# Spreading the output units of a graph-attention kernel over more of its edge steps, and a drain on GpSimd

## The chip, the cores and the metric

The kernel runs on one core of one Trainium2 chip. The core's engines are TensorE (PE, with its weight loads shown as PEld), VectorE (DVE), ScalarE (ACT), GpSimd (POOL) and SyncE (SP, which here only issues DMAs); each works through its own queue in order, and the queues meet through semaphores. The metric is the device time of one execution in microseconds (us), given as the median of several runs.

## The reference

One layer of graph attention over 12,500 nodes and 400,000 edges, with the edges sorted by their target node. The targets are dense at low node numbers: node index grows as the square of the place in the edge list, so half of the edges go to the first quarter of the nodes.

```python
h   = relu(layernorm(x))
msg = (h @ w_src + b_src)[src] + (h @ w_dst)[dst]            # E x 128
rad = mlp3(edge_attr_32)                                     # 32 -> 64 -> 64 -> 128, silu
msg = (msg * edge_weight * rad) @ w_sep + b_sep              # 8 heads x (16 alpha + 16 value)
score = einsum(smooth_leaky_relu(alpha), alpha_dot)          # E x 8
att   = segment_softmax(score, dst)
agg   = segment_sum(value * att, dst)                        # 12500 x 128
out   = x + agg @ w_proj + b_proj
```

## The kernel before, in words

**Setup.** `x` is normalised and multiplied by the two node matrices, and the tables `t_src` and `t_dst` are stored to DRAM (line L335). Meanwhile SP loads weights and a few single words of `dst`: `load_limits` (L243 to L251) fetches, among others, one word per output unit. From these the kernel finds out whether every node of a unit is complete when the unit is begun; if not, it takes a slow path that sorts the edges.

**Edge steps.** The edges are cut into 782 sections of 512, and two sections make a step `k`; there are 391 of them (`NP`), followed by 12 steps that only empty the pipeline. The function `step(k)` issues, in an order written out by hand, pieces of many pipeline stages: the loads of edge weights, targets and target rows some steps ahead; the gathers of step `k+2` on GpSimd (`gather`, L1013: eight indirect DMAs, each with the `t_src` rows of 128 edges); the MLP of steps `k+1` and `k+2`; in step `k` TensorE's transposes of the gathered rows (`sources`, L1073), the multiplication by the radial weights (`radial`, L1062, once in each step, and `message`, L1090); the scores of step `k-1`; the softmax of groups of eight steps (at `k % 8` of 2 and 3); and for step `c = k-12` (`LAG`) the weighted values (L1228), their sums by node (`sums`, L1241 and L1245) and SP's stores of the sums to DRAM (`store`, L1253, into `agg`; `store_win`, L1249). Every 32 steps a "block" repairs nodes that are split between sections (lines L1361 to L1436). The gathers have five buffers for each section of a step (`GSB`), so GpSimd can be three steps ahead of TensorE before it has to wait for a buffer.

**Output units.** The final stage (quotient, projection, residual) is cut into 23 units of 512 nodes (`UNITS`, `UNIT`). Unit `u` begins at step `306 + 4u` (`U0`), the last at step 394, and is spread over three steps: at `q = 0` SP loads its rows of `agg` and of `x` (`load_unit`, L1298; `load_x`, L1303); at `q = 1` VectorE adds the bias and forms the quotients (`unit_bias`, `unit_quotients`, L1307 to L1315); at `q = 2` TensorE transposes (`unit_turn`, L1321, with ScalarE's copy L1323), multiplies by `w_proj` (`unit_product`, L1329), VectorE adds `x` (`unit_out`, L1335) and SP stores the rows of `out` (L1336). The transposes and the product use the PSUM bank `m1`, which the MLP, the scores and the softmax of the same step also use. The buffers of a unit (`gu`, `xs`, `qT`, `ru`) are single.

**The end.** Behind the last gathers of `t_src`, GpSimd gathers rows of `x` for the last 13 steps (`rows_dx`, L1455), loads the block results (L1636, L1638), adds the bias (L1642) and gathers further rows of `x` (`rows_x`, L1449). Its next work is the scatter of finished rows to `out` (`direct_scatter`, L1282; `scatter`, L1440). The first of these scatters is issued only behind the store of the last unit, in step 396 (`late_out`), since it overwrites rows that the units have written.

Of the kernel before, what the change touches and what calls it, by code (L numbers as in the profile page):

```python
# [21 lines left out]
P = 128  # L22
# [16 lines left out]
SEC = T * TS  # L39
# [6 lines left out]
AHEAD = 13  # L46
UNIT = 512
UNITS = 23
U0 = 306
DIRECT = 13  # L50
GSB = 5

# [2 lines left out]
def gnn_kernel(ctx: ExitStack, tc: tile.TileContext, a: dict, out: bass.AP):  # L55
    nc = tc.nc
    x, src, dst = a["x"], a["src"], a["dst"]
    ea, ew = a["edge_attr_32"], a["edge_weight1"]
    N, E = x.shape[0], src.shape[0]
# [3 lines left out]
    NS = -(-E // SEC)  # L63
# [25 lines left out]
    def done(k):  # L89

        return 2 * (k - LAG - 2) + 2

    D = NP - DIRECT
    IN_AGG = done(U0 + 4 * (UNITS - 1)) // 2
    assert D < IN_AGG and done(U0 + 4 * (UNITS - 1)) < NS and UNITS * UNIT + P * 4 >= N - UNIT
    NF = N // P
    tail = N - NF * P
    assert NB == NF + 1
# [80 lines left out]
    with tc.tile_pool(name="node", bufs=2) as np_, tc.tile_pool(name="node1", bufs=1) as n1, \  # L179
# [57 lines left out]
        lim = n1.tile([1, UNITS + 3], I32, name="lim")  # L237
# [5 lines left out]
        def load_limits():  # L243

            with nc.allow_non_contiguous_dma(reason="single targets"):
                at = dst[done(U0) * SEC:done(U0) * SEC + 1]
                nc.sync.dma_start(out=lim[:, 0:UNITS], in_=bass.AP(at.tensor, at.offset, [[1, 1], [8 * SEC, UNITS]]))
                nc.sync.dma_start(out=lim[:, UNITS:UNITS + 1], in_=dst[EARLY * SEC:EARLY * SEC + 1].unsqueeze(0))
                nc.sync.dma_start(out=lim[:, UNITS + 1:UNITS + 2],
                                  in_=dst[(NS - 1) * SEC:(NS - 1) * SEC + 1].unsqueeze(0))  # L250
                nc.sync.dma_start(out=lim[:, UNITS + 2:UNITS + 3], in_=dst[2 * D * SEC:2 * D * SEC + 1].unsqueeze(0))  # L251
# [297 lines left out]
        for i in range(Q):  # L549
# [12 lines left out]
            if i == 1:  # L562
                load_targets()
                load_limits()
# [20 lines left out]
        for i in range(Q - 10, Q):  # L585
            q = i - (Q - 10)
# [321 lines left out]
    def windows():  # L908
# [7 lines left out]
        with tc.tile_pool(name="ps", bufs=1, space=PSUM) as pp, \  # L916
# [33 lines left out]
            def prep_make(u):  # L950
                ri, rb = made[u]
                rows = lp.tile([P, P], F32, name="rows", bufs=1)
                rf = lp.tile([P, 1], F32, name="rf", bufs=1)
                nc.vector.tensor_copy(rf, rb)
                nc.vector.tensor_copy(rows[:T, :], ri[:T, 0, :])
                rel[u] = sp.tile([P, T], F32, name="rel")
                nc.vector.tensor_scalar(rel[u], ri[:, 1, 0:T], rf, None, op0=ALU.subtract)
                made[u] = rows
# [179 lines left out]
            def load_sm(m):  # L1138
                sms[m] = sp.tile([MQ, SEC + 1], BF16, name="sm")
                at = same[0:1, m * MQ * SEC:m * MQ * SEC + 1]  # L1140
                nc.sync.dma_start(out=sms[m], in_=bass.AP(at.tensor, at.offset, [[SEC, MQ], [1, SEC + 1]]))
# [106 lines left out]
            def store_win(c):  # L1248
                nc.sync.dma_start(out=win[c * P:(c + 1) * P, :], in_=accs[c])  # L1249

            def store(c, f):
                at = nc.sync.value_load(base[0:1, f, c:c + 1])
                nc.sync.dma_start(out=agg[ds(at, W - 1), :], in_=accs[c][f * W:(f + 1) * W - 1, :])  # L1253
# [90 lines left out]
            def width(g):  # L1344
                return min(P, NE - g * P)
# [101 lines left out]
            def rows_x(g):  # L1447
                w = width(g)
                nc.gpsimd.indirect_dma_start(  # L1449
                    out=xe_at(g)[:w, :], out_offset=None, in_=x[:, :],  # L1450
                    in_offset=bass.IndirectOffsetOnAxis(ap=ids[:w, g:g + 1], axis=0),
                    bounds_check=N - 1, oob_is_err=False)
# [12 lines left out]
            def xe_at(g):  # L1465
                return big["xe", g // TS][:, g % TS, :]
# [9 lines left out]
            def has(k):  # L1476
                return 0 <= k < NP
# [7 lines left out]
            def step(k):  # L1485
                c = k - LAG
                if has(c - 2) and k <= NP:
                    store_win(c - 2)
                    if c - 2 < IN_AGG:
                        store(c - 2, 0)  # L1490
# [11 lines left out]
                if has(k) and k % MP == 4:  # L1502
                    load_sm(k // MP)
                if has(c - 2) and k <= NP and c - 2 < IN_AGG:
                    store(c - 2, 1)
# [3 lines left out]
                    prep_make(0)  # L1509
                if k % 16 == 7 and has(k + 9):  # L1510
                    prep_make((k + 9) // 16)
                u, q = divmod(k - U0, 4)
                unit = 0 <= u < UNITS
                if unit and q == 0:
                    load_unit(u, sp)
                    load_x(u, sp)
# [40 lines left out]
                if has(c - 1):  # L1557
                    sums(c - 1)
                    if k >= NP:
                        if k == NP + LAG:  # L1560
                            last_rows_2()
                        else:
                            store_win(c - 1)
                        if c - 1 < IN_AGG:
                            store(c - 1, 0)
# [52 lines left out]
            for k in range(-5, NP):  # L1618
                step(k)
                if k == NP - 4:  # L1620
                    block_load(last - 1)
                if k == NP - 2:
                    block_maxima(last - 1)
                    block_nodes(last)
                if k == NP - 1:
                    block_factors(last - 1)
# [6 lines left out]
            for c in range(D, NP):  # L1633
# [3 lines left out]
                                in_=obs_d[0:g0 * P, :].rearrange("(g p) c -> p g c", p=P))  # L1637
            nc.gpsimd.dma_start(out=big["ye", 1][:, 0:(last - 1 - g0) * C].rearrange("p (g c) -> p g c", c=C),  # L1638
                                in_=obs_d[g0 * P:(last - 1) * P, :].rearrange("(g p) c -> p g c", p=P))
            for i in range(-(-DIRECT // TS)):  # L1640
                n = min(TS, DIRECT - i * TS)
                nc.gpsimd.tensor_tensor(big["xw", i][:, 0:n, :], big["xw", i][:, 0:n, :],  # L1642
                                        b_out.unsqueeze(1).to_broadcast([P, n, C]), op=ALU.add)
            for g in range(NC):
                rows_x(g)

            def sum_rows():
                for g in range(0, last - 1, TS):
                    n = min(TS, last - 1 - g)
                    v = big["ye", g // 8][:, g % 8 * C:(g % 8 + n) * C].rearrange("p (g c) -> p g c", c=C)  # L1650
                    nc.gpsimd.tensor_tensor(v, v, big["xe", g // TS][:, 0:n, :], op=ALU.add)
# [31 lines left out]
            for k in range(NP, NP + LAG + 1):  # L1683
                step(k)
                if k - NP in jobs:
                    jobs[k - NP]()
# [83 lines left out]
    with tc.If(unfit == 0) as fit:  # L1770
        windows()
# [70 lines left out]
```

## Time and profile before

| | us |
|---|---|
| median of 3 runs | 4093.39 |
| lowest, highest run | 4090.29, 4094.85 |
| the profiled execution | 4088.26 |
| its span, first to last instruction | 4086.4 |
| PE busy | 3863.1 (95%) |
| DVE busy | 3100.8 (76%) |
| POOL busy | 3061.4 (75%) |
| ACT busy | 1864.5 (46%) |

The profiled execution is 5.1 us below the median and has 1.9 us around its span. In the profile each group of instructions has a line of the kernel, an engine, the tile written and the tiles read, a count, the busy time and the mean time of one, and then the idle time of the engine in front of it with what ended that idle time. "issue" is time in which the engine waited for nothing that the profile shows. The timeline gives start and duration of single instructions in us from the span's start. The line "L1013 ... x3021" counts the gathers into the tiles `gs`; 72 further gathers of the first steps go into other buffers.

### The profile page before, as it was taken

What the parts mean: (1) busy time and instruction counts of PE and PEld (TensorE: products, weight loads), DVE (VectorE), ACT (ScalarE), POOL (GpSimd) and SP (SyncE); (2) the same over time, 40 slices, a digit from 0 to 9 for tenths busy, and PEclk for the clock granted to TensorE, in tenths of its full rate; (3) what the DMA queues carried; (4) which work ended last, traced back from release to release, by engine and by line L of the source; (5) the groups of instructions that cost most, each with busy time, mean ns of one, the idle gap of its engine ahead of it and who ended that gap; (6) DMA issues with size and microseconds to landing.
All of it is one profiled execution on the core that took longest, in us unless ns stands there. A gap on an engine that the chain in (4) does not pass through costs nothing.

```text
span 4086.4 us, 84243 instructions
## 1 busy us (share of the span) xinstructions
PE 3863.1 (95%) x27811; PEld 2347.4 (57%) x27811; DVE 3100.8 (76%) x5557; ACT 1864.5 (46%) x3782; POOL 3061.4 (75%) x3244
## 2 busy tenths in 40 slices
PE   7899999999999999999999999999999999999996
PEld 6356555655555555555555555555555565555555
DVE  7677777777777777777777777777777788777876
ACT  5454444444454444444444444444444444444441
POOL 6777777777777777777777777777777777777775
PEclk9999999999999999999999999999999999999998
DMA  7777777777677776776767676777767777777761
GB/s 248 209 189 195 178 199 189 182 189 185 183 177 190 186 185 169 193 191 173 184 184 189 172 187 186 189 177 186 183 180 191 200 202 200 200 205 202 197 183 53
DMA packets 536556, 762.20 MB, mean 187 GB/s; under 512 B 126721, under 2 KB 339747, under 8 KB 535984
## 3 DMA queue, kind: packets, MB, share of 16 engines
q1 hardware_dynamic: 378120, 498.27, 41.9%
q0 software_dynamic: 101872, 207.34, 24.0%
q10 hardware_dynamic: 56120, 51.10, 4.4%
q8 instruction: 226, 3.70, 0.4%
q14 instruction: 218, 1.79, 0.2%
HBM read 632.27 MB, written 125.70 MB: 185 GB/s over the span
## 4 chain that ended last, share of the span: by engine, by line
PE 66%; DMA 11%; POOL 9%; issue 6%; DVE 5%; SPq 2%; ACT 2%; ACTq 0%; DVEq 0%; POOLq 0%
PE V L1228 14%; PE pa L1096 13%; PE misc L1241 8%; DMA gs<-t_src,idx 8%; POOL gs L1013 7%; PE p L1057 6%; PE pm L1073 6%; PE m L1029 5%; PE pm L1085 4%; PE p L1042 4%; PE m L1113 3%; POOL mT L1013 2%; DMA agg<-ob 1%; DVE mT L1090 1%; DMA win<-ob 1%
## 5 line engine op out<-in xcount | busy, mean ns | idle before, releaser
L1013 POOL DMA_INDIRECT gs<-t_src,idx x3021 | 2871.6, 951 | 922.2 <-issue 774.0
L1098 ACT ACTIVATE sl<-pa,c_b_a 128x512 f32<-128x512 f32 x782 | 537.5, 687 | 1085.1 <-PE pa L1096 1083.3
L1103 DVE SCALAR_TENSOR_TENSOR al<-pa,sl 128x512 f32<-128x512 f32 x782 | 536.8, 686 | 524.0 <-ACT sl L1098 512.3
L1228 PEld LDWEIGHTS V<-c_w_v,mT 128*128 128x128 f32 x6154 | 755.4, 193 | 300.8 <-DVE ob L1245 124.1
L1228 PE MATMUL V<-c_w_v,mT 128*128 128x128 f32 x6154 | 888.0, 288 | 0.0
L1096 PE MATMUL pa<-mT,c_w_a 128*128 128x512 f32 x1564 | 835.1, 616 | 20.9 <-DVE mT L1090 18.6
L1230 DVE TENSOR_TENSOR pvx<-V,Pem 128x512 f32<-128x512 f32 x770 | 528.4, 686 | 222.3 <-PE V L1228 206.6
L1073 PEld LDWEIGHTS pm<-ident,gs 128*128 128x128 f32 x3021 | 373.6, 141 | 495.5 <-issue 470.1
L1044 ACT ACTIVATE h<-p,b 128x512 f32<-128x512 f32 x391 | 469.2, 1200 | 399.5 <-PE p L1042 332.9
L1062 DVE SCALAR_TENSOR_TENSOR rad<-p,c_fc_b,w_b 128x1024 f32<-128x1024 f32 x391 | 500.8, 1281 | 122.2 <-PE p L1057 105.0
L1073 PE MATMUL pm<-ident,gs 128*128 128x128 f32 x3021 | 458.1, 274 | 76.9 <-DMA gs<-t_src,idx 76.4
L1241 PEld LDWEIGHTS misc<-pvx,oh 128*64 128x64 f32 x6250 | 352.4, 137 | 295.9 <-ACT h L1032 286.5
L1090 DVE SCALAR_TENSOR_TENSOR mT<-pm,c_b_src,rad 128x1024 f32<-128x1024 f32 x391 | 497.5, 1272 | 7.1 <-PE pm L1085 6.3
L1241 PE MATMUL misc<-pvx,oh 128*64 128x136 f32 x6250 | 452.2, 287 | 0.4 <-ACT h L1032 0.3
L1057 PE MATMUL p<-h,w3b 64*128 64x512 f32 x1564 | 408.6, 600 | 0.4 <-ACT h L1044 0.4
L1029 PE MATMUL m<-eT,w1b 64*128 64x256 f32 x782 | 277.3, 435 | 19.7 <-ACT qT L1323 14.2
L1085 PE MATMUL pm<-ohT,m 64*128 64x512 f32 x1564 | 287.7, 446 | 0.0
L1032 ACT ACTIVATE h<-misc,b 128x256 f32<-128x256 f32 x391 | 185.4, 474 | 214.4 <-PE misc L1029 198.5
L1029 PE MATMUL misc<-eT,w1b 64*128 64x256 f32 x782 | 277.3, 435 | 0.0
L1096 PEld LDWEIGHTS pa<-mT,c_w_a 128*128 128x128 f32 x1564 | 237.4, 192 | 68.3 <-DVE mT L1090 36.6
L1129 ACT ACTIVATE Sp<-m,b_s 128x512 f32<-128x512 f32 x192 | 131.8, 686 | 311.5 <-PE m L1113 311.5
L1042 PE MATMUL p<-h,w2b 64*64 64x256 f32 x3128 | 261.5, 405 | 0.5 <-DVE rad L1062 0.5
(216 smaller groups left out, 3542.0 us busy)
## 6 DMA issues: line engine op xcount, KB each, us to landing
w_b<-in_edge_weight SPq DMA_DIRECT2D x390, 512.0 KB
d_b<-in_dst SPq DMA_DIRECT2D x390, 256.0 KB
e_t<-in_edge_attr ACTq DMA_DIRECT2D x386, 128.0 KB
sc_d<-Sp SPq DMA_DIRECT2D x192, 256.0 KB
gs<-t_src,idx POOLq DMA_INDIRECT x3021
win<-ob SPq DMA_DIRECT2D x390, 68.0 KB
agg<-ob SPq DMA_DIRECT2D x762, 33.5 KB
md<-t_dst SPq DMA_DIRECT2D x782, 32.0 KB
```

The lines of the kernel that those rows point to most:

```text
L1013: sent = [nc.gpsimd.indirect_dma_start(out=gs[:, t, :], out_offset=None, in_=t_src[:, :], in_offset=bass.IndirectOffsetOnAxis(ap=idx[:, t0 ...
L1029: nc.tensor.matmul(p1[f], w1b[s, :], eTs[k][s, :], start=True, stop=True)
L1057: nc.tensor.matmul(p3[:, f, 0:SEC], w3b[s, :], h2s[k][s, :], start=True, stop=True)
L1062: nc.vector.scalar_tensor_tensor(rad[:, 0:n], p3.rearrange("c f e -> c (f e)")[:, 0:n], b3, w_g[k][:, 0:n], op0=ALU.add, op1=ALU.mult)
L1073: turned = [nc.tensor.matmul(pm[:, t * T:(t + 1) * T], gs[:, t, :], ident, start=(t == 0), stop=False, is_transpose=True, skip_group_check ...
L1090: nc.vector.scalar_tensor_tensor(mTs[k][:, 0:n], pms.rearrange("c f e -> c (f e)")[:, 0:n], b_n, rad[:, 0:n], op0=ALU.add, op1=ALU.mult)
L1096: nc.tensor.matmul(pa[:, 0:n], w_a, mTs[k][:, f * SEC:f * SEC + n], start=True, stop=True)
L1098: nc.scalar.activation(sl[:, 0:n], pa[:, 0:n], AF.Silu, bias=b_a, scale=1.0)
L1103: nc.vector.scalar_tensor_tensor(al, pa, 0.25, sl, op0=ALU.mult, op1=ALU.add)
L1228: nc.tensor.matmul(V[:, t, :], mTs[c][:, o:o + T], w_v, start=True, stop=True)
L1230: nc.vector.tensor_mul(pvx[c][:, f, 0:n, 0:C].rearrange("p t (h k) -> p t h k", h=H), V[:, 0:n, :].rearrange("p t (h k) -> p t h k", h=H), ...
L1241: nc.tensor.matmul(acc[f * W:(f + 1) * W, :], ohs[c][:, f * TS + t, :], pvx[c][:, f, t, :], start=(t == 0), stop=(t == n - 1), skip_group_ ...
```

## The change

The units no longer begin at every fourth step from 306 on. Four runs of steps are given instead: 96, 128, 160 and 192; then 204 to 282 by 13; then 296 to 386 by 10; then 390 and 394. The count of units, their work and the steps of the last two or three (386, 390, 394) stay as they are. `load_limits` fetches its words with four DMAs in place of one, since the steps no longer have one stride. In the end part one `drain` is issued on GpSimd between its last gathers of `x` and what follows them.

```diff
-U0 = 306
+UNIT_RUNS = ((96, 32, 4), (204, 13, 7), (296, 10, 10), (390, 4, 2))
+UNIT_STEP = [a + i * d for a, d, n in UNIT_RUNS for i in range(n)]
...
-                at = dst[done(U0) * SEC:done(U0) * SEC + 1]
-                nc.sync.dma_start(out=lim[:, 0:UNITS], in_=bass.AP(at.tensor, at.offset, [[1, 1], [8 * SEC, UNITS]]))
+                u = 0
+                for k, d, n in UNIT_RUNS:
+                    at = dst[done(k) * SEC:done(k) * SEC + 1]
+                    nc.sync.dma_start(out=lim[:, u:u + n], in_=bass.AP(at.tensor, at.offset, [[1, 1], [2 * d * SEC, n]]))
+                    u += n
...
-                u, q = divmod(k - U0, 4)
-                unit = 0 <= u < UNITS
+                unit = k >= UNIT_STEP[0]
+                u = max((i for i, a in enumerate(UNIT_STEP) if a <= k), default=0)
+                q = k - UNIT_STEP[u]
                 if unit and q == 0:
                     load_unit(u, sp)
                     load_x(u, sp)
...
             for g in range(NC):
                 rows_x(g)
+            nc.gpsimd.drain()
```

More of the change, by code (lines that the diff above doesn't have):

```diff
@@ L93, in gnn_kernel @@
     D = NP - DIRECT
-    IN_AGG = done(U0 + 4 * (UNITS - 1)) // 2
-    assert D < IN_AGG and done(U0 + 4 * (UNITS - 1)) < NS and UNITS * UNIT + P * 4 >= N - UNIT
+    IN_AGG = done(UNIT_STEP[-1]) // 2
+    assert UNITS == len(UNIT_STEP) and min(b - a for a, b in zip(UNIT_STEP, UNIT_STEP[1:])) >= 3
+    assert D < IN_AGG and done(UNIT_STEP[-1]) < NS and UNITS * UNIT + P * 4 >= N - UNIT
     NF = N // P
```

## The prediction

> **What bounds the kernel now.** The page first: what is busy, and the group that stands on top.
>
> ```profile
> PE 3863.1 (95%) x27811; PEld 2347.4 (57%) x27811; DVE 3100.8 (76%) x5557; ACT 1864.5 (46%) x3782; POOL 3061.4 (75%) x3244
> L1013 POOL DMA_INDIRECT gs<-t_src,idx x3021 | 2871.6, 951 | 922.2 <-issue 774.0
> ```
>
> PE looks like the bound. But GpSimd's 25% of idle time is nearly all "issue", some 0.3 us ahead of each gather, so its gathers may run without a real wait. So second: the gathers of L1013 in three stretches (length, busy time, count; then clock and DMA). The first lies well before the units, the second in the middle, the third holds 20 of the 23 units.
>
> ```profile
> 282.00:864.00 582.00, 440.61 (x465) 1.00 0.73 191
> 1060.00:3060.00 2000.00, 1513.72 (x1594) 0.98 0.71 184
> 3145.00:3945.00 800.00, 605.63 (x638) 1.00 0.76 201
> ```
>
> One gather starts every 2000/1594 = 1.255 us in the second stretch, every 800/638 = 1.254 us in the third: the same pace with units and without, and 10.03 us for the eight gathers of a step. Third, the pace of the steps. L1062 runs once in each step, so first and last start over the count give it, in the first stretch, in 2260 to 3060 and in the third.
>
> ```profile
> L1062 DVE SCALAR_TENSOR_TENSOR rad<-p,c_fc_b,w_b x60: 1268/1284/1285, 289.1 to 854.8; 128x1024 f32<-128x1024 f32 x60
> L1062 DVE SCALAR_TENSOR_TENSOR rad<-p,c_fc_b,w_b x80: 1266/1284/1285, 2260.8 to 3054.8; 128x1024 f32<-128x1024 f32 x80
> L1062 DVE SCALAR_TENSOR_TENSOR rad<-p,c_fc_b,w_b x79: 1264/1283/1285, 3144.8 to 3941.0; 128x1024 f32<-128x1024 f32 x79
> ```
>
> That is 565.7/59 = 9.59, 794.0/79 = 10.05 and 796.2/78 = 10.21 us a step. In the first stretch gathers made ahead are being used up, and the steps run at their own pace of 9.59. In the middle they follow GpSimd (10.03). With a unit every fourth step they follow neither: they are slower than GpSimd, and fall behind it. What PE's transposes wait for says the same; the first row is of 2260 to 3060, the second of the third stretch.
>
> ```profile
>   DMA gs<-t_src,idx: 29.8, 28
>   DMA gs<-t_src,idx: 9.1, 31
> ```
>
> How far the steps fall behind is seen from the last gather of a step and the same step's L1062. GpSimd's gathers of `t_src` end at 3973.85 with the five of step 390; counting back from there, 3957.42 is the last gather of step 388 and 2992.37 that of step 292, three 32-step block cycles before.
>
> ```profile
> 2992.37 0.94 POOL L1013 DMA_INDIRECT gs<-t_src,idx  x1 [0.30 <-issue]
> 2997.02 1.28 DVE L1062 SCALAR_TENSOR_TENSOR rad<-p,c_fc_b,w_b 128x1024 f32<-128x1024 f32 x1 [1.43 <-PE p L1057]
> 3957.42 0.94 POOL L1013 DMA_INDIRECT gs<-t_src,idx  x1 [0.30 <-issue]
> 3972.60 1.28 DVE L1062 SCALAR_TENSOR_TENSOR rad<-p,c_fc_b,w_b 128x1024 f32<-128x1024 f32 x1 [1.30 <-PE p L1057]
> 3973.85 0.94 POOL L1013 DMA_INDIRECT gs<-t_src,idx  x1 [0.30 <-PE misc L1241]
> ```
>
> The lag is 4.65 us at step 292 and 15.18 at step 388. So the kernel is GpSimd's gathers, at a fixed pace from some 91 us on, plus the lag at their end, plus the tail. The 10.53 us by which the lag grew are what the units' old place costs.
>
> **The units moved.** What one of them puts on the engines, from the groups in the third stretch (20 units):
>
> ```profile
> L1329 PE MATMUL m<-c_w_proj,qT 128*128 128x128 f32 x160 | 21.1, 275 | 0.0
> L1321 PE MATMUL m<-ident,gu 128*128 128x128 f32 x80 | 12.0, 273 | 0.0
> L1315 DVE TENSOR_TENSOR gu<-gu,ru 128x512 f32<-128x512 f32 x20 | 13.8, 691 | 0.7
> L1335 DVE TENSOR_TENSOR xs<-m,xs 128x512 f32<-128x512 f32 x20 | 13.8, 689 | 0.0
> L1307 DVE TENSOR_TENSOR xs<-xs,c_b_proj 128x512 f32<-128x512 f32 x20 | 13.7, 683 | 1.4 <-DMA xs<-in_x 1.3
> L1323 ACT COPY qT<-m 128x512 f32<-128x512 f32 x20 | 11.7, 586 | 3.6 <-PE m L1321 2.4
> ```
>
> PE gets 33.1/20 = 1.66 us a unit, DVE (three groups shown) 2.07, ACT 0.59. The price on the steps is read from their pace: (10.21 - 9.59) x 4 = 2.5 us a unit; from below, wait that PE no longer had (29.8 - 9.1 = 20.7) and lag gained (10.5), over 20 units, give 1.6. I take 2.5, since it holds the stalls as well. The slack behind GpSimd is 10.05 - 9.59 = 0.46 us a step: 1.8 us between units four steps apart, 4.6 at ten steps and 6.0 at thirteen. So a unit is absorbed before the next begins, and at nothing as long as its cover, the wait for gathers, is there; without cover it would be 2.5 us.
>
> Eleven units now meet other users of bank `m1` in their third step: those begun at a multiple of 8 (96, 128, 160, 192, 256, 296, 336, 376) meet the softmax, those at 217, 243 and 269 the scores. Before, none did. PE then waits for a scan, and the scan behind it for the unit's addition.
>
> ```profile
> 3136.36 1.21 DVE L1150 TENSOR_TENSOR_SCAN M<-m,S 128x512 f32<-128x512 f32 x1
> ```
>
> That is at most 1.21 + 0.69 = 1.9 us more, 4.4 us for such a unit, just under the 4.6 of ten steps. For the lag at the end only 376 matters.
>
> On SP, each unit has three DMAs, and waits of its own:
>
> ```profile
> SPq L1298 <- DMA agg<-ob: 36.8, 19, 2.8
> SPq L1336 <- DVE xs L1335: 33.8, 11, 4.8
> SPq L1253 <- DMA gu<-agg: 8.2, 8, 1.6
> ```
>
> Over 20 units that is 78.8/20 = 3.9 us each, in front of the stores and of the loads of weights, targets and target rows behind them. The step issues those loads two or more steps before their use, 20 us, so at nothing; if that lead were gone, 3.9 us a unit, which at ten steps still lies beside GpSimd. The unit's traffic is the same, only earlier.
>
> **What is left at the end.** Without units the lag at step 388 would be as at step 292, 4.65. The unit of 386 has gone through two of its three steps by then: I add 1.5 of its 2.5. Of unit 376 (2.5 to 4.4) the eight steps 380 to 387 pay back 8 x 0.46 = 3.7: 0 to 0.7 is left, and I take 0. So the lag at 388 is 6.2 instead of 15.18, a gain of 9.0 (8.3 to 10.5, the upper end with no trace of 386 either). From there on both kernels have the same steps, units 390 and 394 among them, and gathers that are already there.
>
> **The tail, and the drain.** The end must come from the steps and not from GpSimd:
>
> ```profile
> 4014.03 0.97 POOL L1449 DMA_INDIRECT gs<-in_x,ids  x1 [0.30 <-PE p L1267]
> 4035.68 0.34 SPq L1336 DMA_DIRECT2D out<-xs  x1
> 4038.57 1.03 POOL L1282 DMA_INDIRECT out<-gs,ids_d  x1 [23.57 <-DVE dq L1262]
> 4074.16 0.91 POOL L1440 DMA_INDIRECT out<-w_b,ids  x1 [0.30 <-DVE w_b L1669]
> ```
>
> GpSimd is done with its gathers of `x` at 4015.0 and waits 23.57 us. The row names DVE, but the last condition is the store of the last unit, issued at 4035.68; then its scatters run to 4075 with 0.3 us between them. With everything in the steps 9.0 us earlier the wait shrinks to 14.6. The drain lies in it. No row prices it on GpSimd: its lower end is 0, and the upper end in which it is hidden is 14.6. I take 0, as nearest to it stands the last gather, 0.97 us long, which is all that is still at work. Behind the drain stand the scatters, and nothing else waits for it.
>
> **Setup.** `load_limits` has three more DMAs on SP, ahead of the stores of `t_src`.
>
> ```profile
> 30.49 0.63 SPq L247 DMA_DIRECT2D lim<-in_dst  x1
> 31.65 0.23 SPq L249 DMA_DIRECT2D lim<-in_dst  x1
> 84.28 0.32 SPq L335 DMA_DIRECT2D t_src<-ms  x1
> 91.19 0.94 POOL L1013 DMA_INDIRECT mT<-t_src,idx  x1 [3.87 <-issue]
> SPq L335 <- ACT ms L327: 17.8, 8, 10.0
> ```
>
> 3 x 0.23 to 3 x 0.63 = 0.7 to 1.9 us of SP. The gathers begin at 91.19 behind the last stores, and any delay there goes through the whole kernel. But SP waits for ACT's results 17.8 us in all, so most is hidden; bounds 0 to 1.9, I take 0.4.
>
> **Sum.** 9.0 - 0.4 = 8.6 us less: span 4086.4 - 8.6 = 4077.8, profiled execution 4088.26 - 8.6 = 4079.7. That execution was 5.1 us under the median of the runs, so for the median 4093.39 - 8.6 = 4084.8. 0.2% of the median is 8.2 us, about what a measurement of this kernel can tell from no change; the forecast lies just beyond.
>
> **Rivals.** *The lag comes back.* The units at 366, 376 and 386 meet the block work of steps 366 to 375 and the softmax, and less is paid back than the mean slack says. For it: the slack of 0.46 us is a mean, and heavy steps use it first. If the last two units leave all of their 2.5 + 4.4 us, the lag at 388 is 11.6 and the gain 3.6, less 0.4: 4090.2, no change that can be told. Against: ten steps bring 4.6.
>
> *Slower: the units hold up GpSimd.* Where PE was behind, a stretched gather cost nothing; in the new places GpSimd sets the pace, and whatever stretches a gather counts in full. L1307 and L1315 take 0.69 us each with both inputs in SBUF. If each held the gathers for its whole length, the 20 units moved would cost 20 x 1.38 = 27.6, net 19.0 slower: 4112.4. It decides from 8.6/20 = 0.43 us a unit. Against it: the pace of 1.255 us without units and 1.254 with one every fourth step; 1.38 us a unit would have made the latter 1.255 + 1.38/32 = 1.298.
>
> The Trainium skill, "SBUF — State Buffer", section "SBUF: two separate sides", states this rule: VectorE and GpSimd share a port pair, which is locked for a whole instruction, among others when VectorE has two inputs in SBUF and GpSimd reads SBUF. By that rule the units would come out at this rival's time; the equal pace in the trace does not bear it out for these gathers.
>
> *The drain does not end with the gathers.* If it lasted over 14.6 us, the scatters would start late by the excess, and over 23.2 us the kernel would be slower. Nothing in the profile is that long on GpSimd; at 14.6 + 8.6 + 10 us it would be 4103.4.
>
> *More is gained.* No trace of unit 386, no cost in setup, and fewer collisions of GpSimd's additions with DVE in the tail: 10.5 to 12, so 4082.
>
> **How the numbers follow.** Forecast 0.60, of which 0.38 beyond 8.2 us and 0.22 within, as its bounds are 6.4 (8.3 - 1.9) to 10.5; lag comes back 0.15; units hold up GpSimd 0.07; drain 0.05; more gained 0.13. Faster 0.38 + 0.13 = 0.51, same 0.22 + 0.15 = 0.37, slower 0.12. The range reaches from 4081 (a gain of 12) to 4094, which takes in the lag's return and the spread of the runs and leaves out most of the slower cases; the forecast's own range is 4082.9 to 4087.0.
>
> **What would show it.** Right: steps from 2260 on and from 3145 on both at 10.05 us; the lag at step 388 near 6; PE's wait for gathers near 20 us in the third stretch; GpSimd's gathers still 1.255 us apart; its wait ahead of the first scatter near 15 us; the first gather of `t_src` at 91 to 92. Wrong: a slower pace of the gathers, a lag over 10 at step 388, or a tail that does not move with the lag because a transfer or the scatters hold it.

## The result and the profile after

The changed kernel takes 4086.5 us (median of 22 runs, 4078.3 to 4089.5) against 4093.2 us of the kernel before, run beside it (22 runs, 4087.4 to 4100.5). The ratio is 0.9983, with a 95% interval of 0.9976 to 0.9989: 6.7 us less (4.5 to 9.8). That is a gain, though a smaller one than the 0.2% that the prediction took as its bound. The forecast was 4084.8. The profiled execution of the changed kernel took 4089.07 us, 2.6 above its median, and that of before 4088.26, 5.1 below its median; so the two traces stand 0.8 us the wrong way round, and are compared part by part and not by their ends. Lines of the changed kernel are 5 higher than before's from L250 on, and 7 higher at its end.

From the page of the changed kernel, the busy times and the group of the gathers:

```profile
PE 3865.2 (95%) x27811; PEld 2349.3 (57%) x27811; DVE 3104.5 (76%) x5557; ACT 1862.3 (46%) x3782; POOL 3065.6 (75%) x3244
L1018 POOL DMA_INDIRECT gs<-t_src,idx x3021 | 2875.4, 952 | 923.0 <-issue 768.5
```

As before, GpSimd waits 0.3 us between gathers and for nothing else. The steps, by the rows of L1067 (L1062 of before) in 2260 to 3060 and in 3145 to 3945 (count, shortest, median and longest duration, first and last start), and what TensorE's transposes of gathered rows wait for in the second of these stretches:

```profile
L1067 DVE SCALAR_TENSOR_TENSOR rad<-p,c_fc_b,w_b x80: 1266/1284/1285, 2262.9 to 3051.4; 128x1024 f32<-128x1024 f32 x80
L1067 DVE SCALAR_TENSOR_TENSOR rad<-p,c_fc_b,w_b x78: 1265/1284/1285, 3153.1 to 3936.6; 128x1024 f32<-128x1024 f32 x78
  DMA gs<-t_src,idx: 9.5, 25
```

That is 9.98 us a step in the first stretch and 783.5/77 = 10.18 in the second, where before had 10.05 and 10.21. With a unit every ten steps the steps are still slower than GpSimd, and TensorE's wait for gathers is 9.5 us as it was 9.1 before, not the 20 of the forecast. The lag at step 388, read as in the prediction, is 12.19 us against 15.18.

The points at which one kernel's time can be set against the other's are the first and the last gather of `t_src`, L1067 of the last edge step (390), and the last scatter. From the timeline of the changed kernel:

```profile
93.89 0.94 POOL L1018 DMA_INDIRECT mT<-t_src,idx  x1 [2.97 <-DMA t_src<-ms]
3981.30 0.94 POOL L1018 DMA_INDIRECT gs<-t_src,idx  x1 [0.30 <-PE m L1334]
3995.21 0.88 DVE L1067 SCALAR_TENSOR_TENSOR rad<-p,c_fc_b,w_b 128x640 f32<-128x640 f32 x1
4046.14 1.03 POOL L1287 DMA_INDIRECT out<-gs,ids_d  x1 [23.75 <-DVE dq L1267]
4081.73 0.91 POOL L1445 DMA_INDIRECT out<-w_b,ids  x1 [0.30 <-issue]
```

and of before, for the two that the prediction does not show (the span's ends are 4086.4 and 4087.2):

```profile
3990.99 0.88 DVE L1062 SCALAR_TENSOR_TENSOR rad<-p,c_fc_b,w_b 128x640 f32<-128x640 f32 x1
```

| part of the span, us | before | after | difference |
|---|---|---|---|
| A: start to first gather | 91.19 | 93.89 | +2.70 |
| B: first to last gather | 3882.66 | 3887.41 | +4.75 |
| C: last gather to L1062 of step 390 | 17.14 | 13.91 | -3.23 |
| D: from there to the end of the last scatter | 84.08 | 87.43 | +3.35 |
| E: from there to the end of the span | 11.33 | 4.56 | -6.77 |

The forecast put the whole gain into C. C did shrink, by a third of what was expected, and A and D took it back. What is left of the gain is E, which the forecast had at nothing. Most of E is GpSimd's own drain at the end of the program. Its rows (shortest, median, longest of three in ns; first and last start), of before and then of after, with the added drain:

```profile
L1839 POOLq DRAIN  x3: 46/106/8714, 4076.8 to 4086.1; - x3
```

```profile
L1652 POOLq DRAIN  x1: 14801/14801/14801, 4014.1 to 4014.1; - x1
L1846 POOLq DRAIN  x3: 46/106/3272, 4083.1 to 4086.9; - x3
```

The added drain begins at 4014.12 while gathers of `x` still run, and ends at 4028.92, 6.53 us behind the end of the last of them (4022.39). The scatters come at 4046.14, so it is hidden. The drain at the program's end is 5.4 us shorter, and begins 0.46 us behind the last scatter instead of 1.8. So 5.4 of the 6.8 us in E are the shorter drain; the other 1.3 lie ahead of it and, as the run of the moved units alone will show, come without the added drain too.

### The profile page after: what moved, and what is told of

Its sections match the earlier page's. It is cut to its first block, busy times and chain, and to the rows that moved or that the text cites. A ratio compares the mean times of both kernels' runs of the same rounds, so it can differ in the third digit from the quotient of the medians.

```text
span 4087.2 us, 84249 instructions
## 1 busy us (share of the span) xinstructions
PE 3865.2 (95%) x27811; PEld 2349.3 (57%) x27811; DVE 3104.5 (76%) x5557; ACT 1862.3 (46%) x3782; POOL 3065.6 (75%) x3244
## 4 chain that ended last, share of the span: by engine, by line
PE 68%; DMA 12%; POOL 7%; issue 5%; DVE 5%; ACT 2%; SPq 1%; ACTq 0%; DVEq 0%; POOLq 0%
PE V L1233 15%; PE pa L1101 14%; DMA gs<-t_src,idx 8%; PE misc L1246 8%; PE pm L1078 7%; PE p L1062 6%; POOL gs L1018 6%; PE m L1034 5%; PE pm L1090 4%; PE p L1047 4%; PE m L1118 3%; DMA agg<-ob 1%; DVE mT L1095 1%; POOL mT L1018 1%; DMA win<-ob 1%
## 5 line engine op out<-in xcount | busy, mean ns | idle before, releaser
L1067 DVE SCALAR_TENSOR_TENSOR rad<-p,c_fc_b,w_b 128x1024 f32<-128x1024 f32 x391 | 500.5, 1280 | 105.6 <-PE p L1062 87.3
L1062 PE MATMUL p<-h,w3b 64*128 64x512 f32 x1564 | 405.9, 596 | 0.5 <-ACT h L1049 0.4
L1217 DVE TENSOR_TENSOR oh<-lane,misc 128x504 f32<-128x504 f32 x391 | 261.2, 668 | 0.1
```

The costliest lines, as they stand in the source:

```text
L1062: nc.tensor.matmul(p3[:, f, 0:SEC], w3b[s, :], h2s[k][s, :], start=True, stop=True)
L1067: nc.vector.scalar_tensor_tensor(rad[:, 0:n], p3.rearrange("c f e -> c (f e)")[:, 0:n], b3, w_g[k][:, 0:n], op0=ALU.add, op1=ALU.mult)
```

## The experiments

There were twelve runs of seven kernels. In ten of them the profiled execution had a granted clock of 0.919 to 0.928, and before itself took 5281 to 5299 us there; each run is compared with before on its own chip in the same job, and the two at a clock of 0.986 and 0.988 (before 4096) are the ones that speak for the measured case. At the lower clock the gathers take as long (949 to 952 ns) and wait more than twice as long, so they do not set the pace there; of the kernel with the drain alone (its first run):

```profile
L1013 POOL DMA_INDIRECT gs<-t_src,idx x3021 | 2868.0, 949 | 2061.4 <-issue 748.5
```

Theory A is the forecast: the smaller lag is the gain, the drain brings nothing. Theory B: the drain takes over most of the last drain, and the moved units come out near nothing, because of what they cost elsewhere.

**The drain alone,** before with one line:

```diff
             for g in range(NC):
                 rows_x(g)
+            nc.gpsimd.drain()
```

> The kernel before with the drain alone: units from step 306 on, one DMA for the units' words. Theory A (the forecast: the gain is the smaller lag of the steps behind GpSimd's gathers, and the drain is hidden and brings nothing): ratio 1.000, the lag at step 388 near 15 us, GpSimd's last drain of the program near 8.7 us as before. Theory B (the drain in the gap takes over work of the drain with which the program ends, 8.71 us in the profile before and 3.27 after): 5.4 us less, ratio 0.9987, the last drain near 3.3 us, the lag unchanged at 15.

> The kernel before with the drain alone behind GpSimd's last gather of x; the same kernel as the first drain run, wanted on a chip whose granted clock is near 0.98, where the gathers set the pace. Theory A, the forecast (the drain stands in a gap and brings nothing): within 2 us of before, 4093, and GpSimd's drain at the program's end stays near its 8.7 us. Theory B (the drain takes over what the program's last drain does): that last drain falls from 8.71 us to 2 to 3.3 us and the time by as much, 4087 to 4088. If the chip is again one at a clock of 0.92, only the length of the last drain can be read.

It was run twice, both times at the lower clock: 0.9992 (0.9973 to 1.001; 5282.9 against 5291.1 us) and 1.000 (0.9976 to 1.0024; 5281.7 against 5281.4). These times cannot tell 6 us from nothing. The drains can be read, first run and second (the added one and the last ones):

```profile
L1646 POOLq DRAIN  x1: 14879/14879/14879, 5171.5 to 5171.5; - x1
L1840 POOLq DRAIN  x3: 46/106/2238, 5274.1 to 5276.9; - x3
```

```profile
L1840 POOLq DRAIN  x3: 46/106/2242, 5277.7 to 5280.5; - x3
```

The last drain falls to 2.24 us, as theory B has it, and the added one again ends 6.53 us behind the last gather of `x`. 6.53 + 2.24 = 8.77, within 0.06 us of the 8.71 that the last drain takes alone, which fits work that is only done earlier; with the 3.27 of the changed kernel the sum is 9.80, so this is not shown to hold exactly. In all kernels with the drain the end of the last scatter lies 4.5 to 5.0 us ahead of the span's end; without it 10.2 to 11.5. So the last drain is shorter without the moved units too. What the drain alone does to the time was not measured at the higher clock.

**The moved units alone,** the changed kernel without its drain. First on the two chips at the lower clock, under these expectations (first and second run):

> The changed kernel without its drain: units in their new places, four DMAs for their words. Theory A: all of the gain, 6 to 8 us, ratio 0.998 to 0.9985, the last drain near 8.7 us. Theory B: the lag at step 388 falls by 3 us as in the profile after (12.2 against 15.2), and the setup gives back 0 to 2.7 us of it; together 0 to 3 us, ratio 0.9993 to 1.000, the last drain 8.7 us.

> The changed kernel without the drain: the moved units and their four limit loads. Theory A: it carries the whole gain, 4093 - 8.6, about 4085 to 4087, last drain 8.7 us. Theory B: it carries what is left of the 6.7 us when 5.4 us are the drain's, 4091 to 4093, because the limit loads start the first gather of t_src 2.2 us late and VectorE waits up to 5 us for rows of x at units that lie outside steps 2 and 6 of 8; the last drain is 8.7 us.

1.0026 (1.0008 to 1.0043) and 1.0038 (1.0018 to 1.0058): slower than before by 14 us each time. Then on a chip at 0.986:

> The changed kernel without the drain, once more, for a chip at a granted clock near 0.98 (4093 us before). Theory A, the forecast: the moved units carry the gain, 4093 - 8.6, about 4085. Theory B: the runs so far show 11.3 to 11.6 us from the end of the last scatter to the end of the span without the drain and 4.6 to 4.9 with it, which is the whole of the 6.7 us, so the units and their limit loads come out at nothing: 4092 to 4095, and the last drain is 8.71 us. On a chip at 0.92 the two runs of this kernel so far were 14 us over before, and a third would be the same.

4093.0 us against 4096.0 (11 and 15 runs): 0.9994, 95% interval 0.9983 to 1.0005. The forecast's 8.6 us would be 0.9979, which lies outside; no change at all lies inside. This interval and the changed kernel's (0.9976 to 0.9989) overlap a little, so it is the trace, more than the times, that gives the rest of the gain to the drain. The last drain has its old length:

```profile
L1845 POOLq DRAIN  x3: 46/106/8713, 4079.2 to 4088.5; - x3
```

By parts this execution has A +1.83, B +3.25, C -5.72, D +4.15, E -1.13 against before. So the lag does shrink when the units are moved, by less than forecast, and A and D give it back. Part E is 10.2 us here, and the changed kernel's 4.56 make the added drain worth 5.6 us. Three things, each with its rows, lie behind what A and D give back and what C falls short of. First, on SP's queue, the limit loads of before (shown in the prediction, 0.63 us for the one) and of after:

```profile
30.48 2.83 SPq L251 DMA_DIRECT2D lim<-in_dst  x4
34.46 0.84 SPq L340 DMA_DIRECT2D t_src<-ms  x2
```

The first stores of `t_src` follow at 34.46 instead of 32.27, and the first gather comes 2.7 us later. The prediction had 0.4 us for it, since SP waits for ScalarE 17.8 us in the setup. Those waits absorb the delay only for a while: the store at 52.62 in before is 0.5 us later in after, but the last one ahead of the gathers (87.84 in before) is 2.5 us later.

Second, VectorE waits for a unit's rows of `x` ahead of `unit_bias`, the longest time at the unit of step 356. From the timeline of the changed kernel, the two loads and that wait, and then for the tile `xs` of the whole run the wait of the changed kernel, of the units alone and of before (us, times):

```profile
3661.31 0.35 SPq L1303 DMA_DIRECT2D gu<-agg  x1
3661.71 0.42 SPq L1308 DMA_DIRECT2D xs<-in_x  x1
3665.69 0.69 DVE L1312 TENSOR_TENSOR xs<-xs,c_b_proj 128x512 f32<-128x512 f32 x1 [5.37 <-DMA xs<-in_x]
```

```profile
  DMA xs<-in_x: 12.3, 6
```

```profile
  DMA xs<-in_x: 21.5, 6
```

```profile
  DMA xs<-in_x: 1.3, 2
```

Before's units all begin at `k % 8` of 2 or 6. In the new places five begin at 3, 4 or 5 (those of steps 204, 243, 269, 316 and 356), and these have 11.9 of the 12.3 us and 20.6 of the 21.5; there SP issues the unit's loads late, and VectorE stands still in its own queue. What this costs at the end is not shown: the units alone have more of this wait, and yet the smaller lag at step 390 (11.43 against 13.91). Something else sets the changed kernel's trace apart. TensorE's granted clock fell to about half in five stretches of its steps between 3145 and 3945, 27 us in all; in before this happened once there, for 3.4 us, and with the units alone three times, for 13.7. Two of the five, beside the units at 306 and 356, with ten us ahead of the first, and then before's one (length; busy time of PE, PEld, DVE, ACT, POOL; clock, DMA share, GB/s):

```profile
3150.00:3160.00 10.00, 8.85 (x71) 4.97 (x70) 9.77 (x20) 7.30 (x12) 7.56 (x9) 1.00 0.75 101
3165.00:3172.00 7.00, 6.33 (x32) 3.89 (x32) 1.51 (x3) 1.43 (x3) 5.48 (x6) 0.53 0.63 204
3666.00:3673.00 7.00, 3.86 (x10) 2.51 (x11) 5.99 (x13) 1.52 (x4) 5.17 (x7) 0.53 0.91 250
```

```profile
3722.00:3726.00 4.00, 3.98 (x15) 2.86 (x16) 1.09 (x3) 1.81 (x6) 3.08 (x4) 0.57 0.99 229
```

How much of the lag these stretches make, and how much the waits ahead of them, is not shown. Third, in part D, VectorE is held beside GpSimd's four adds of the bias row. From the changed kernel's timeline of both engines, and VectorE's row of before for the first of the two instructions:

```profile
4000.97 4.29 POOL L1648 TENSOR_TENSOR gs<-gs,c_b_proj 128x512 f32<-128x512 f32 x4
4000.34 3.33 DVE L1393 TENSOR_TENSOR de<-up,cuts 128x128 f32<-128x128 f32 x1
4003.71 1.25 DVE L1394 TENSOR_TENSOR de<-de,up 128x128 f32<-128x128 f32 x1
```

```profile
3996.13 0.33 DVE L1388 TENSOR_TENSOR de<-up,cuts 128x128 f32<-128x128 f32 x1
3996.49 1.24 DVE L1389 TENSOR_TENSOR de<-de,up 128x128 f32<-128x128 f32 x1
```

An instruction of 0.3 us took 3.33. With a smaller lag VectorE comes to these instructions when GpSimd begins its adds; in before it came to them as the second add ended. Over their usual lengths VectorE's instructions are held 0.95 us in before, 3.99 in after and 3.0 with the units alone. If all of it counts, that is 3.0 of after's 3.35 us in part D, but only 2.1 of the 4.15 with the units alone, where the rest stays open. The Trainium skill, "SBUF — State Buffer", section "SBUF: two separate sides", says that VectorE and GpSimd share a port pair, which one of them locks for a whole instruction, among others when VectorE has two inputs in SBUF and GpSimd reads SBUF. Here the trace agrees, with 3.33 us in place of 0.33; but 3.0 us is more than two of the adds last (1.3 us each), and before's L1388 ran at its usual 0.33 us in the midst of such adds, so it is not held every time.

**The limit loads alone,** before's units with its one load cut into four (of 4, 7, 10 and 2 words):

> The kernel before with the units' words fetched by four DMAs in place of one, and nothing else. If the later first gather of t_src in the profile after (93.9 against 91.2 us) comes from these DMAs, the first gather is near 93 to 94 us here and the time 1 to 2.7 us longer, ratio 1.0003 to 1.0007. If it is the spread of executions: first gather at 91 to 92 us, ratio 1.0000.

1.0009 (0.9993 to 1.0025), at the lower clock: 4.4 us more, not told from nothing. The trace shows the step itself again: 2.85 us for the four loads, the first stores of `t_src` at 34.74, and the first gather at 101.49. All traces at the lower clock bear this out: with four loads (three traces) the first gather comes at 98.8 to 101.5 us, with one or two (seven traces) at 95.6 to 97.2. So the four loads do delay the gathers, by 1.6 to 5.9 us from trace to trace there.

**Units in other places.** First every eighth step from 226 to 378, then 386, 390 and 394, with the drain and two limit loads; then every eighth step throughout, with one limit load:

```diff
-UNIT_RUNS = ((96, 32, 4), (204, 13, 7), (296, 10, 10), (390, 4, 2))
+UNIT_RUNS = ((226, 8, 20), (386, 4, 3))
```

> The changed kernel with its units at steps 226 to 378 by eight (all of them 2 above a multiple of 8), then 386, 390, 394, and two DMAs for their words. In the profile after VectorE waited up to 5.4 us for the rows of x of the units at 316 and 356, which SP issued 8 to 11 us into the step; the units before the change all stood at 2 or 6 above a multiple of 8 and had at most 1.0 us. If the place in the cycle of eight is what makes the unit's loads late: no wait over 1.1 us ahead of a unit's bias, the lag at step 388 at 7 to 9 us instead of 12.2, and 3 to 5 us less than the changed kernel (ratio to before 0.9972 to 0.9978). If the spacing sets the lag: eight steps leave more than ten, the lag at 388 is 12 or more and the ratio 0.998 or above.

```diff
-UNIT_RUNS = ((96, 32, 4), (204, 13, 7), (296, 10, 10), (390, 4, 2))
+UNIT_RUNS = ((218, 8, 23),)
```

> The changed kernel with the units at 218, 226, ... 394, every eighth step: one limit load in place of four, all units at step 2 of 8, the drain kept. Theory A: as after, since the lag at step 388 is again 5 to 8 us against the 15.2 of before, 4084 to 4087. Theory B: the first gather back at its time of before (2.2 us earlier than after), no wait over 1 us for the rows of x ahead of a unit's VectorE work, and the drain's 5.4 us: 4080 to 4083, the fastest of all.

The first gave 0.9973 (0.9951 to 0.9994). The second was run three times, all at the lower clock: 0.9960 (0.9940 to 0.9980), 0.9955 (0.9932 to 0.9978) and 0.9958 (0.9940 to 0.9976), 19 to 26 us less than before. So there the place of the units is worth far more than the drain: the same units at after's places, without the drain, were 14 us slower than before. The wait for rows of `x` is not the reason at that clock, since it is 0 in the first and 4.3 us in the second trace of the units alone there. The later runs went in under these expectations:

> Units at 218, 226, ... 394, one limit load in place of four, the drain kept; for a chip at a granted clock near 0.98. Theory A: as after, 6 to 9 us under before. Theory B: the drain gives 6.5 us as in after, and what the units lost there comes on top: the first gather of t_src 2.2 us earlier than after, no wait over 1 us for rows of x ahead of a unit's VectorE work, lag of step 388 at 5 to 8 us (12.2 after, 15.2 before): 10 to 14 us under before, ratio 0.9966 to 0.9976, below after's 0.9983. If the units are worth nothing wherever they stand, it comes out at 0.9983 as after.

> Once more the units at 218, 226, ... 394 with one limit load and the drain, for a chip at a granted clock near 0.98. Theory A: 6 to 9 us under before, as after. Theory B: the drain's 6.5 us and on top 4 to 7 us that the units bring when their limit load delays nothing and they stand at step 2 of 8: ratio 0.9966 to 0.9976. Units worth nothing anywhere: 0.9983.

**Before without its first 20 units:**

```diff
-                unit = 0 <= u < UNITS
+                unit = 20 <= u < UNITS
```

> The kernel before with the first 20 of the 23 units left out, so that the rows of the output that they write stay unwritten (part of the computation is missing). It bounds what any placing of the units can bring. Theory A: the lag of the last steps stays at 5 to 8 us instead of 15.2, 4083 to 4086. If the lag grows towards step 388 without the units too, the units are not its cause and the time stays at 4091 to 4094. The last drain stays 8.7 us in every theory.

0.9978 (0.9955 to 1.000) at the lower clock, 13.6 us less. With all its units at every eighth step the kernel gained 19 to 26 us, of which some 6.5 are the drain's (part E is 4.7 to 5.0 us with it and 11.3 to 11.5 without in the traces at this clock), so in those places the units cost nothing that shows there; the intervals, about 11 us to each side, would hide a few us. For the higher clock this stays without a run.

**All that the traces pointed to:** units every eighth step from 218, one limit load, the drain, and GpSimd's adds spread between the gathers of `x`:

```diff
-            for i in range(-(-DIRECT // TS)):
-                n = min(TS, DIRECT - i * TS)
-                nc.gpsimd.tensor_tensor(big["xw", i][:, 0:n, :], ...)
             for g in range(NC):
                 rows_x(g)
+                i = g // 3
+                if g % 3 == 2 and i < -(-DIRECT // TS):
+                    n = min(TS, DIRECT - i * TS)
+                    nc.gpsimd.tensor_tensor(big["xw", i][:, 0:n, :], ...)
             nc.gpsimd.drain()
```

> The every-eighth kernel with the drain, and GpSimd's four adds of the bias row spread between its gathers of x (behind the third, sixth, ninth and twelfth) instead of standing in a row ahead of them. In the runs at a clock of 0.985 VectorE's instructions beside those four adds were held 0.95 us (before), 3.99 us (after) and 3.0 us (units alone). Theory B: at such a clock no VectorE instruction of the last 100 us is held by more than 1.1 us, no wait for rows of x ahead of a unit's work, the limit loads take 0.6 us of SP's queue in place of 2.83, and the last drain is 2.2 to 3.3 us: 10 to 14 us under before, ratio 0.9966 to 0.9976. Theory A: 6 to 9 us under before, as after. At a clock of 0.92 the every-eighth kernel was at 0.9955 to 0.9960 and this one would be the same, since its steps run 50 us behind the gathers and no VectorE work was held beside the adds there.

At a clock of 0.988: 4076.1 us against 4096.1 (5 and 9 runs), ratio 0.9951, 95% interval 0.9937 to 0.9964. That is 20 us less than before, more than either theory had, and its interval lies below the changed kernel's (0.9976 to 0.9989). Its rows from the timeline, with the longest hold of VectorE (usually 0.7 us), and then its last drains:

```profile
30.82 0.62 SPq L251 DMA_DIRECT2D lim<-in_dst  x1
92.08 0.94 POOL L1018 DMA_INDIRECT mT<-t_src,idx  x1 [4.16 <-issue]
3978.78 0.94 POOL L1018 DMA_INDIRECT gs<-t_src,idx  x1 [0.31 <-issue]
3988.48 0.88 DVE L1067 SCALAR_TENSOR_TENSOR rad<-p,c_fc_b,w_b 128x640 f32<-128x640 f32 x1
4013.21 1.29 DVE L1169 TENSOR_TENSOR M<-S,M 128x512 f32<-128x512 f32 x1
4068.09 0.92 POOL L1445 DMA_INDIRECT out<-w_b,ids  x1 [0.30 <-issue]
```

```profile
L1847 POOLq DRAIN  x3: 46/106/2238, 4070.5 to 4073.3; - x3
```

Against before: A +0.89, B +4.04, C -7.44 (9.70 us), D -3.55, E -6.79, together the 12.9 us by which its span of 4073.5 is shorter. No instruction of VectorE waits for rows of `x`. Part D also has one unit less, since none begins at 390. How much of D the spread adds alone bring, and how much the missing unit, was not run apart.

**What stays open.** B is 3.3 to 4.8 us longer in all three later traces than in before's, whatever the places of the units. Before's trace is of an execution 5.1 us under its median, and over all runs the mean of these 3021 gathers lies between 949 and 952 ns, where 1 ns makes 3 us; among them 949 and 952 stand for before's own places, and 952 for 20 units left out. So I take most of B for a spread between executions, but it is not shown what spreads it. A part of B is the units' own. Gathers that run beside a unit's bias addition and quotients on VectorE, whose inputs lie in SBUF, are in part stretched, the longest to 1.6 us; here is one of the unit at 306 in the changed kernel:

```profile
3154.27 1.53 POOL L1018 DMA_INDIRECT gs<-t_src,idx  x1 [0.30 <-issue]
3154.26 0.68 DVE L1312 TENSOR_TENSOR xs<-xs,c_b_proj 128x512 f32<-128x512 f32 x1
```

Over the usual 0.944 to 0.945 us such gathers are 2.1 us longer in all in before (47 gathers, 23 units), 3.5 in after, 2.8 with the units alone and 5.0 in the last kernel, so 0.7 to 2.9 us of B. Beside the addition `unit_out`, of the same length but with one input in PSUM, none in these four traces is longer than 0.954. It is also not shown why the steps at the lower clock cost 12.7 us and depend so much on the units' places.

## Why the prediction was right, and where it was not

The number was right (4084.8 forecast, 4086.5 measured, inside the forecast's own range of 4082.9 to 4087.0), and so was the sign. The reasons were not: the sum had two large errors that nearly cancel, a gain from the lag that was too large and a gain from the drain that it did not have. That the number came out is luck.

- *GpSimd's gathers set the pace.* Right at the clock of the measured case: 952 ns each, 0.3 us between them. The rival that the units hold them up falls at its price (4112.4, from 1.38 us a unit), but not as such: the gathers beside a unit were stretched by 3.5 us over 23 units, 0.15 each, of which before's places had 2.1. The equal pace that the prediction read against it could not show so little.
- *"The drain ... I take 0."* Wrong, and with the lag the largest error: the last drain is 5.4 us shorter, and part E 5.6 us below that of the units alone. The bounds ran from 0 to 14.6 us of cost and had no gain in them. The row that would have told it stood in before's trace, the 8.71 us of GpSimd's last drain at the end of the program (8714 in the rows above); I had followed the tail only to the last scatter at 4075 and not asked what the 11.3 us behind it are. The rival "the drain does not end with the gathers" was right that it goes on, by 6.53 us, and these lie in the gap.
- *"A unit is absorbed before the next begins."* Half wrong. Taken from L1067's starts, as the time of a unit's six steps over the median of unit-free steps at the same place in 16 (steps 20 to 385), the units at `k % 8` of 0, 1, 2 and 6 cost 0.1 to 3.8 us (the one at 306, with the clock at 0.53 beside it, 8.1), about the forecast's 2.5; those at 204, 243, 269, 316 and 356 cost 2.9 to 6.4. With the units alone it is 1.1 to 3.2 and, for those five, 4.4 to 8.7. The slack of 0.46 us a step, 4.6 in ten, does not pay the dear ones back before the next begins, and the third stretch ran at 10.18 us a step, not 10.05.
- *SP's part "at nothing", since its loads lead by 20 us.* Here is one error in that step: the prediction reckoned only with the loads behind the unit's, of weights and targets, but the unit's own rows of `x` are loaded in the step ahead of their use, and VectorE waited 12.3 us for them. The other is that the prediction did not reckon with TensorE's clock, which in the third stretch stood at half for 27 us. Which of the two made the lag is not shown.
- *The lag.* Gain 9.0 forecast at step 388, 3.0 measured there (15.18 to 12.19) and 3.2 at step 390 (17.14 to 13.91). The rival "the lag comes back" (gain 3.6, 4090.2) had this size right; that its cause, the block work and the softmax beside the last units, was at work is not shown.
- *"From there on both kernels have the same steps."* Wrong by 3.35 us. The prediction named GpSimd's adds as a collision that would become smaller; moving the lag moved VectorE's work into them, and they held it 3.0 us more.
- *Setup, 0.4 us of 0 to 1.9.* Measured 2.7 in this pair of traces and 1.8 with the units alone, about or above the upper bound: the one load, cut into four, took 2.83 us of SP in place of 0.63, and the waits for ScalarE hid that only for a while. Some of it is spread, since the last kernel, with one load, has +0.89.

Put together, without B: A + C + D is +2.8 us, E is -6.8, the sum -4.0; measured 6.7 less, with an interval that begins at 4.5. For the units alone the same sum gives -0.9 (measured -3.0), for the last kernel -16.9 (measured -20.0). Each lies 2 to 3 us short of what was measured, in the direction in which before's quick execution would put it.

## What to carry to other kernels

Follow the tail to the end of the span and not to the last useful instruction: what an engine has to clear up at the end can be done earlier, in a gap of its own queue. When work is moved to other steps, look in those steps at when its loads are issued, and at what it or the work behind it will meet on shared engines; a mean slack does not tell that. And a forecast that comes out right has not been tested until each of its parts is read from the trace.

## What the hardware showed that was not expected

- A drain on GpSimd is not free behind this kernel's indirect DMAs: 8.71 us at the end of the program in six traces without an earlier drain, equal to within 1 ns (0.17 to 0.18 us at the program's start, ahead of all of them); with an earlier one, 6.53 us behind the last gather there and 2.24 to 3.27 at the end. The Trainium skill, "VectorE: DVE Perf Modes", section "The DRAIN you can't avoid", speaks of drains of some 12 ns at the begin and end of a program, alike on all engines; here the other engines' are 7 to 91 ns, and GpSimd's is not, and the measurement decides.
- Beside four adds in a row on GpSimd an instruction of VectorE took 3.33 us in place of 0.33. The other way round, some of GpSimd's gathers took up to 1.6 us in place of 0.94 beside VectorE's instructions with both inputs in SBUF.
- TensorE's granted clock fell to about half for 3.4 or 6.8 us at a time in the steps, five times in the third stretch of the changed kernel and once in that of before.
- The same kernel took 4093 to 4096 us in the jobs at a granted clock of 0.985 to 0.988 and 5281 to 5299 in those at 0.92; the moved units without the drain made no difference that can be told in the first and were 14 us slower in the second.
